# One exponential and four small transposes placed later in the queues of a four-layer graph kernel

## The chip, the cores and the metric

The kernel runs on one core of a Trainium2 chip. The metric is the device time of one execution in microseconds (us). Before the change three runs gave 1911.79, 1900.36 and 1915.36 us, a median of 1911.79. The profile is one execution more, of 1882.29 us. Line numbers (L1753) are those of the kernel before. PE is TensorE, DVE VectorE, ACT ScalarE, POOL GpSimd, and SP SyncE, which issues most of the transfers.

## The reference

A matrix `x` of 2708 rows (nodes) and 256 columns goes through four layers, each a graph part and a feed-forward part with residual additions. Two of the parts matter here.

Layer 2's graph part is attention with one head. Cut to the essentials:

```python
h = x @ W.T
a_src = (h * attn_src).sum(axis=-1)
a_dst = (h * attn_dst).sum(axis=-1)
scores = a_src[None, :] + a_dst[:, None]
mask = (adj > 0).astype(h.dtype)
s = jnp.where(scores > 0, scores, ALPHA * scores) * mask
e = jnp.exp(s - jnp.max(s, axis=1, keepdims=True)) * mask
out = (e / (jnp.sum(e, axis=1, keepdims=True) + 1e-08)) @ h
```

Its feed-forward part routes all rows to the same two of eight experts, `gelu(x @ W1 + b1) @ W2 + b2`, and normalizes the sum with `x`. Layer 3's graph part is the same kind of attention with four heads of 64 columns, and its feed-forward part one product with a bias.

## The kernel before

The rows lie in SBUF as `x`, 22 tiles of 128 rows (the last has 20). The layers follow each other, and each layer's start is worked into the end of the one before. All arithmetic is float32. The order of the work on each engine comes out of a scheduler that takes the program's order and the dependencies; `engine_after` and `in_order` (L152 to L167) add ordering edges without a wait, by which an instruction is kept behind another one of its engine. ACT, DVE, POOL and SP each work through their instructions in the order that results.

**Layer 2's front** (L1570 to L1685). The tiles are taken in groups of 2, 4, 4, 4, 4, 4 (`FOURS`). For each group:

- `turned_up` loads what layer 1's experts gave for those tiles (`mine`, transfers issued by SP), adds it to `x` (L1588, by DVE for the early groups and by POOL for tiles 14 to 21), transposes `x` on PE into a `ps_tmp` buffer of PSUM (L1596), and ACT copies that to SBUF (L1598). There are three `ps_tmp` buffers.
- `valued` multiplies by the weights (L267, into one of five `ps_acc` buffers), ACT copies the two score columns (`sc`, L1639), takes exponentials of them (L141), and DVE writes the values `hh` (L1649). The scores' tile `sc` is cleared by a memset (L1628), for the later groups on POOL.
- `row_scores` transposes the group's scores on PE (L1497), ACT copies them out (L1499), and SP stores them to DRAM (L1500).
- `row_factor` (L1507) reads them back, broadcast to all partitions (`row_read`, L1504), into the group's stretch of `Rb`, and takes the exponential of the stretch in place on ACT (L141 through `lnexp`).

The main loop (L1735 to L1778) then forms on DVE, for each tile of sources, `e = max(Rb, G) * mask` (L1745), and PE multiplies `e` with `hh` (L1753) for five columns of tiles at a time.

**Layer 2's feed-forward part and layer 3's front** (L1944 to L2055). The rows are taken in six parts: four of 512, one of 384 and one of 276. For each part, `units` runs the first products (L375, 32 matmul records per part, eight PSUM results) and the gelus on ACT (L377), and `outputs` the second products (L1962, into `ps_acc`). Between them `finish` normalizes the part before (L1978 on ACT, L1991 to L1993 on DVE). After `outputs`, `front` does layer 3's front for the part before: per tile a transpose (L220) and its copy (L221), the product with layer 3's weights (L267), and three copies on ACT (L2015, L2017, L2018), the last of which writes the scores `sc`; then `row_scores` (L1497, L1499, L1500) for the whole part. `sc` has one buffer; a memset on POOL (L2001) clears it at the beginning of each `front`. First products, transposes, weight products and score transposes all take their PSUM results from three `ps_tmp` buffers in turn.

In the last part (`end`), ACT also loads another table (L135), takes the exponentials of the first stretches of rows (`rows_of`, L1894), and scales the values (L2107); POOL copies corners of the mask (`last_mask`, L1882 to L1887). The last tiles' front is done inside the main loop of layer 3 (L2125 to L2277), whose products are L2219 and L2227 and whose weights `e` come from DVE (L2190).

Of the kernel before, what the change touches and what calls it, by code (L numbers as in the profile page):

```python
# [11 lines left out]
AF = mybir.ActivationFunctionType  # L12
# [3 lines left out]
P = 128  # L16
# [50 lines left out]
def adj_ffn4(ctx: ExitStack, tc: tile.TileContext, a: dict, out: bass.AP):  # L67
    nc = tc.nc
# [71 lines left out]
    def lnexp(out, in_, func, **kw):  # L140
        i = s.activation(out, in_, func, **kw)  # L141
        tc.add_manual_dep(i.ins, pinned[-1].ins.name, mybir.DependencyInfo(
            mybir.DependencyClass.NoSync, mybir.DependencyReason.DATA), reason="table")
# [733 lines left out]
    with ExitStack() as l0:  # L877
# [74 lines left out]
        def front(t0):  # L952

            tiles = range(t0, min(t0 + 2, NT))
            w = (len(tiles) - 1) * P + rows(tiles[-1])
            xT = gp.tile([P, DC, 2 * P], F32, name="xT", bufs=2)
            nc.sync.dma_start(xT[:, :, :w], a["xT"][:, t0 * P : t0 * P + w].rearrange(
                "(c p) t -> p c t", p=P))
            load_tiles(nc, x, tiles, a["x"])
            st = stats(tiles, by_log=True)  # L960
            for i, t in enumerate(tiles):
                r = rows(t)
                p = times(xT, i * P, r, w_sb, D)
                v.scalar_tensor_tensor(msg[:r, t, :], p, st[1][:r, i : i + 1], b_bc[:r],
                                       op0=ALU.mult, op1=ALU.add)
# [11 lines left out]
        for tiles in GROUPS:  # L977
            end = tiles is GROUPS[-1]
# [7 lines left out]
            for j in range(FULL):  # L986
# [33 lines left out]
                for p, pair in zip(acc, pairs):  # L1020
                    for n in pair:
                        if n == len(own):
                            continue
                        _, k, q = own[n]
# [477 lines left out]
    def row_read(dst, kept, h, t0, n):  # L1502

        nc.sync.dma_start(dst.rearrange("p (t c) -> p t c", c=P), kept[t0 : t0 + n, h : h + 1, :]  # L1504
                          .rearrange("t h c -> h t c").to_broadcast([P, n, P]))

    def row_factor(dst, kept, h, t0, n):  # L1507

        row_read(dst, kept, h, t0, n)
        lnexp(dst, dst, AF.Exp, scale=0.8)  # L1510

# [2 lines left out]
    with tc.tile_pool(name="t3", reuse_waits="tile", bufs=1) as t3:  # L1517
# [34 lines left out]
        with tc.tile_pool(name="g2", reuse_waits="tile", bufs=1) as gp:  # L1552
# [10 lines left out]
            def last_of(engines):  # L1563
                had = {}
                for i in nc.cur_bb.bb.instructions:
                    if i.engine in engines:
                        had[i.engine] = i.name
                return had

            def turned_up(tiles):  # L1570

                n, t0 = len(tiles), tiles[0]
                adder = v if t0 < FOURS[4][0] else g
                xT = gp.tile([P, DC, W], F32, name="xT4", bufs=2)
                late = [t for t in tiles if t not in EARLY]
                if late:
                    o = gp.tile([P, 4, D], F32, name="mine", bufs=2)
                    for i in load_tiles(nc, o, late, given[1], t0):
                        behind(i, scattered["given1"])

                def add_two(k):
                    r = rows(t0 + k + 1)
                    for q, m in (((P, 2),) if r == P else ((P, 1), (r, 1))):
                        i = k if q == P else k + 1
                        if t0 + i in EARLY:
                            continue
                        xs = x[:q, t0 + i : t0 + i + m, :]
                        adder.tensor_tensor(xs, xs, o[:q, i : i + m, :], ALU.add)  # L1588

                def turn_two(k):  # L1590
                    r = rows(t0 + k + 1)
                    p = ps_tmp()
                    for i in range(2):
                        q = rows(t0 + k + i)
                        for c in range(DC):
                            te.transpose(p[:, (c * 2 + i) * P : (c * 2 + i) * P + q],  # L1596
                                         x[:q, t0 + k + i, c * P : (c + 1) * P], ident[:q, :q])
                    s.copy(xT[:, :, k * P : (k + 1) * P + r],  # L1598
                           p.rearrange("p (c t) -> p c t", c=DC)[:, :, : P + r])

                def scale():
                    return prepared[t0] if t0 in prepared else stats(tiles, by_log=True)[1]

                for k in range(0, n if len(late) == n else n - len(late), 2):
                    add_two(k)
                    turn_two(k)
                if len(late) in (0, n):
                    rstd = scale()
                    return tiles, xT, lambda i, r: rstd[:r, i : i + 1]

                def add_late():
                    first = len(nc.cur_bb.bb.instructions)
                    for k in range(n - len(late), n, 2):
                        add_two(k)
                    engine_after(first, mybir.EngineType.DVE, last_put[0])

                def turn_late():
                    had, first = last_of(fronts), len(nc.cur_bb.bb.instructions)
                    for k in range(n - len(late), n, 2):
                        turn_two(k)  # L1620
                    for e in fronts:
                        engine_after(first, e, had[e])

                return tiles, xT, (n - len(late), add_late, turn_late)
# [30 lines left out]
                return sc, t0, n  # L1655

            ahead, todo = [turned_up(FOURS[0])], list(FOURS[1:])
            for k in range(len(FOURS)):
                sc, t0, n = valued(*ahead.pop(0))
                had, first = {}, len(nc.cur_bb.bb.instructions)  # L1660
                if ahead and type(ahead[0][2]) is tuple:
                    tiles, xT, (m, _, turn_late) = ahead[0]
                    some = prepared[tiles[0]]
                    begun = scores_of(tiles)
                    begin_values(tiles, xT, lambda i, r: some[:r, i : i + 1], *begun, 1)
                    turn_late()
                    first = len(nc.cur_bb.bb.instructions)
                    others = stats(tiles[m:], by_log=True)[1]
                    engine_after(first, mybir.EngineType.DVE, last_put[0])

                    def rstd(i, r):
                        return some[:r, i : i + 1] if i < m else others[:r, i - m : i - m + 1]

                    ahead[0] = (tiles, xT, rstd, begun)
                    begin_values(tiles, xT, rstd, *begun, len(tiles))
                    had, first = last_of(fronts), len(nc.cur_bb.bb.instructions)
                while todo and len(ahead) < 2:
                    ahead.append(turned_up(todo.pop(0)))
                    if len(ahead) == 1:
                        row_scores(kept, sc[:, :n, 1], t0, n)  # L1680
                for e, past in had.items():
                    engine_after(first, e, past)
                if k > 0:
                    row_scores(kept, sc[:, :n, 1], t0, n)
                row_factor(Rb[:, t0 * P : (t0 + n) * P], kept, 0, t0, n)  # L1685

            spread_out(hh[:, FULL, :])
            spread_out(G[:, FULL, :])
# [223 lines left out]
        with tc.tile_pool(name="h2", reuse_waits="tile", bufs=2) as hp:  # L1912
# [35 lines left out]
            def units(c0, w):  # L1948
                hT = []
                for k in range(2):  # L1950
                    h = hp.tile([P, H2C, W], F32, name="hT", bufs=2)
                    i = hidden(h, xnT, w1[:, k], lambda f: b1s[:, k, f : f + 1], c0, w, H2C)
                    hT.append(h)
                return hT, i
# [71 lines left out]
            def at_once(steps):  # L2026
                for _ in steps:
                    pass

            was = None  # L2030

            parts = CHUNKS[:-2] + [(CHUNKS[-2][0], 3 * P), (CHUNKS[-2][0] + 3 * P, W + CHUNKS[-1][1] - 3 * P)]
            for c0, w in parts:
                own = tiles_of(c0, w)
                end = c0 + w == N
                hT, i = units(c0, w)
                if end:


                    pin(i.ins.name)  # L2040
                    rows_of(0, "both")
                    last_mask()
                    factors(0, was[0][0][0])
                if was is not None:
                    at_once(finish(*was, end))
                y = ypool.tile([P, 4, D], F32, name="y", bufs=2)
                outputs(own, hT, y)
                if was is not None:
                    at_once(front(was[0]))
                    for t in range(NT) if was[0][0][0] == 0 else ():  # L2050
                        r = rows(t)
                        g.tensor_copy(mask[:, t, t * P : t * P + r], diag[:, t, :r])
                if end:
                    factors(was[0][0][0], own[0][0])
                was = (own, y)  # L2055
# [262 lines left out]
```

## Time and profile before

| what | us |
|---|---|
| median of three runs | 1911.79 |
| the profiled execution | 1882.29 |
| its span | 1880.6 |
| PE busy | 1820.4 |
| DVE busy | 1076.1 |
| ACT busy | 656.0 |
| POOL busy | 387.3 |
| layer 2's front, first transpose to first L1753 | 1062.95 to 1095.48 |
| layer 2's main loop | 1095.48 to 1308.02 |
| feed-forward part with layer 3's front, first L375 to first L2219 | 1324.04 to 1507.69 |
| layer 3's main loop from its first L2219 | from 1507.69 |

A line of the timeline gives the start, the duration, the engine, the line of the kernel and the operation, what is written and what is read, and in brackets how long the engine had been idle before it and what ended that. Matmuls of one kind that follow each other are merged (x8), and L267 or L375 count four records per result. A line of the windows gives, for a stretch of time, how long each engine was busy, and at its end the granted clock of PE as a share of full speed, the share of time in which the transfer engines were busy, and GB/s. Times are counted from the span's start.

### The profile page before, as it was taken

What the parts mean: (1) busy time and instruction counts of PE and PEld (TensorE: products, weight loads), DVE (VectorE), ACT (ScalarE), POOL (GpSimd) and SP (SyncE); (2) the same over time, 40 slices, a digit from 0 to 9 for tenths busy, and PEclk for the clock granted to TensorE, in tenths of its full rate; (3) what the DMA queues carried; (4) which work ended last, traced back from release to release, by engine and by line L of the source; (5) the groups of instructions that cost most, each with busy time, mean ns of one, the idle gap of its engine ahead of it and who ended that gap; (6) DMA issues with size and microseconds to landing.
All of it is one profiled execution on the core that took longest, in us unless ns stands there. A gap on an engine that the chain in (4) does not pass through costs nothing. (4 is left out here: it accounts for less than half of the span.)

```text
span 1880.6 us, 25848 instructions
## 1 busy us (share of the span) xinstructions
PE 1820.4 (97%) x9453; PEld 1335.0 (71%) x9453; DVE 1076.1 (57%) x2468; ACT 656.0 (35%) x1474; POOL 387.3 (21%) x460
## 2 busy tenths in 40 slices
PE   8999999999999999999999899998899999999998
PEld 7888788888888888888788788887566733233344
DVE  7687863444333525354642465555445498888877
ACT  8868742222222303113232323223223551132232
POOL 0014254333331001403547310000000100011020
PEclk9999999999998999999999999999899999999999
DMA  8535657877873554544775430000101000022120
GB/s 269 157 104 161 225 177 283 336 301 281 305 272 108 165 150 119 146 113 130 218 235 166 140 70 7 1 1 1 45 1 34 18 1 24 23 28 35 26 35 18
DMA packets 92494, 231.63 MB, mean 123 GB/s; under 512 B 18207, under 2 KB 48967, under 8 KB 84936
## 3 DMA queue, kind: packets, MB, share of 16 engines
q1 hardware_dynamic: 70792, 183.28, 29.8%
q0 software_dynamic: 21568, 46.61, 8.9%
q8 instruction: 78, 1.28, 0.3%
q14 instruction: 56, 0.46, 0.1%
HBM read 218.39 MB, written 30.80 MB: 133 GB/s over the span
## 5 line engine op out<-in xcount | busy, mean ns | idle before, releaser
L2190 DVE SCALAR_TENSOR_TENSOR e<-arena,G,mask 128x1024 f32<-128x1024 f32 (+1 forms) x252 | 275.1, 1151 | 34.1 <-PE den L2227 33.2
L2219 PE MATMUL num<-e,wh 128*64 128x512 f32 (+4 forms) x1056 | 214.1, 549 | 0.7 <-ACT L_gnn_W L1499 0.3
L1753 PE MATMUL ps_acc<-hh,e 128*128 128x257 f32 x882 | 199.2, 382 | 1.7 <-ACT o L1696 1.7
L1025 PE MATMUL acc<-msg,wt 128*128 128x256 f32 x882 | 197.8, 381 | 1.5 <-DVE wt L975 1.2
L1421 PE MATMUL acc<-sup,adrow 128*128 128x256 f32 x882 | 198.3, 382 | 0.7 <-DMA adrow<-in_adjT 0.4
L1421 PEld LDWEIGHTS acc<-sup,adrow 128*128 128x128 f32 x882 | 165.1, 190 | 28.4 <-issue 5.5
L1753 PEld LDWEIGHTS ps_acc<-hh,e 128*128 128x128 f32 x882 | 164.0, 191 | 29.0 <-ACT o L1696 4.3
L1025 PEld LDWEIGHTS acc<-msg,wt 128*128 128x128 f32 x882 | 165.5, 191 | 26.7 <-DVE wt L975 1.8
L615 PE MATMUL ps_acc<-xTs,wa 128*128 128x256 f32 (+1 forms) x768 | 169.9, 374 | 2.8 <-DVE xTs L605 2.7
L617 ACT ACTIVATE hTs<-ps_acc,wa 128x256 f32<-128x256 f32 (+1 forms) x192 | 88.8, 464 | 237.7 <-PE yacc L649 155.6
L649 PE MATMUL yacc<-wb,hTs 128*128 128x256 f32 x736 | 170.6, 384 | 0.1
L615 PEld LDWEIGHTS ps_acc<-xTs,wa 128*128 128x128 f32 x768 | 137.2, 191 | 29.0 <-DVE xTs L605 5.1
L2219 PEld LDWEIGHTS num<-e,wh 128*64 128x64 f32 (+1 forms) x1056 | 70.2, 136 | 122.7 <-issue 105.4
L649 PEld LDWEIGHTS yacc<-wb,hTs 128*128 128x128 f32 x736 | 138.8, 192 | 18.1 <-DVE ys L651 0.5
L1745 DVE SCALAR_TENSOR_TENSOR e<-Rb,G,mask 128x640 f32<-128x640 f32 (+2 forms) x110 | 85.0, 774 | 90.5 <-PE ps_acc L1753 90.4
L1386 DVE TENSOR_SCALAR mask<-adrow 128x1024 uint8<-128x1024 f32 (+1 forms) x66 | 41.6, 630 | 124.1 <-DMA adrow<-in_adjT 123.7
L2227 PE MATMUL den<-e,wh 128*32 128x512 f32 (+4 forms) x1056 | 112.2, 546 | 0.0
L221 ACT COPY xT<-ps_tmp 128x256 f32<-128x256 f32 x76 | 26.8, 366 | 199.1 <-PE ps_tmp L220 198.7
L782 PE MATMUL yacc<-wb,hTs 128*128 128x256 f32 x384 | 90.0, 390 | 0.0
L975 DVE SCALAR_TENSOR_TENSOR wt<-adrow,wt 128x640 f32<-128x640 f32 (+3 forms) x67 | 71.2, 1065 | 25.1 <-ACT wt L141 24.8
L2227 PEld LDWEIGHTS den<-e,wh 128*32 128x32 f32 (+1 forms) x1056 | 33.2, 109 | 73.6 <-issue 69.5
L537 POOL DMA_INDIRECT given<-ys,xs x46 | 65.3, 1420 | 84.0 <-DVE ys L652 68.2
(487 smaller groups left out, 2632.6 us busy)
## 6 DMA issues: line engine op xcount, KB each, us to landing
adhalf<-in_adjT SPq DMA_DIRECT2D x42, 677.0 KB
wb<-in_L_ffn_W2p SPq DMA_DIRECT2D x24, 1152.0 KB
wb<-in_L_ffn_Wdp SPq DMA_DIRECT2D x24, 1152.0 KB
wa<-in_L_ffn_W1b SPq DMA_DIRECT2D x24, 1028.0 KB
adrow<-in_adjT SPq DMA_DIRECT2D x42, 512.0 KB
adrow<-in_adjT SPq DMA_DIRECT2D x42, 320.0 KB
adrow<-in_adjT SPq DMA_DIRECT2D x21, 576.0 KB
adrow<-in_adjT SPq DMA_DIRECT2D x21, 448.0 KB
```

What stands on the lines that cost most here:

```text
L615: i = te.matmul(p[:, f % 2, : m * P], lhsT=w1[:, c, f * P : (f + 1) * P], rhs=xT[:, c, : m * P], start=(c == 0), stop=(c == DC - 1))
L617: s.activation(hT[:, f, : m * P], p[:, f % 2, : m * P], AF.Gelu, bias=bias[:, f : f + 1])
L649: te.matmul(q[:, k, :], lhsT=hT[:, f, k * P : (k + 1) * P], rhs=w2[:, f, :], start=(f == 0), stop=(f == HC - 1))
L782: te.matmul(q, lhsT=hT[:, f, :], rhs=w2[:, f, :], start=(f == 0), stop=(f == HC - 1))
L975: v.scalar_tensor_tensor(wt, ad, 1.0, wt, op0=ALU.is_lt, op1=ALU.mult)
L1025: te.matmul(p[:q, n - pair[0], :], lhsT=wt[:, k : k + q], rhs=msg[:r, j, :], start=(j == 0 and n == pair[0]), stop=(j == FULL - 1 and n == ...
L1421: te.matmul(p[:q, n - pair[0], :], lhsT=ad[:, k : k + q], rhs=sup[:, jj, :], start=(jj == 0 and n == pair[0]), stop=(jj == FULL - 1 and n ...
L1745: i = v.scalar_tensor_tensor(e[:r, :w], Rb[:r, c0 : c0 + w], G[:r, j, :], mask[:r, j, c0 : c0 + w], op0=ALU.max, op1=ALU.mult)
L1753: te.matmul(p[:, : D + 1], lhsT=e[:, k : k + q], rhs=hh[:, j, :], start=(j == 0), stop=False)
L2190: v.scalar_tensor_tensor(e[:, :w], slow[:, m % 2, k, :w], G[:, j, 2 * pair + k, :], mask[:, j, c0 : c0 + w], op0=ALU.max, op1=ALU.mult)
L2219: te.matmul(num[k * DK : (k + 1) * DK, hf, :q], lhsT=wh[some, j, 2 * pair + k, :DK], rhs=e[some, :q], start=(j == 0), stop=(j == FULL), ti ...
L2227: te.matmul(den[z * Q : (z + 1) * Q, :q], lhsT=wh[some, i, 2 * pair + k, DK : DK + 1] .to_broadcast([some.stop - some.start, Q]), rhs=e[so ...
```

## The change

Two places are edited. In layer 2's front, `row_factor` is dissolved: the read of a stretch stays where it was, and its exponential is issued after the next group's `row_scores` (the last group's after the loop). An ordering edge keeps it behind the ACT instruction that was last in the program by then.

In layer 3's front, the generator `front` is run for the part before only up to its last step, the score transpose with its copy and store. That step is run in the next part, after `units`, and an ordering edge keeps the transpose behind the last of `units`' products on PE. In the last part the step is run at once as before, so that it is moved for four of five parts.

```diff
-    def row_factor(dst, kept, h, t0, n):
-
-        row_read(dst, kept, h, t0, n)
-        lnexp(dst, dst, AF.Exp, scale=0.8)
...
             ahead, todo = [turned_up(FOURS[0])], list(FOURS[1:])
+            factor = []
+
+            def factors_of(dst):
+                had, first = last_of(fronts), len(nc.cur_bb.bb.instructions)
+                lnexp(dst, dst, AF.Exp, scale=0.8)
+                engine_after(first, mybir.EngineType.Activation, had[mybir.EngineType.Activation])
+
             for k in range(len(FOURS)):
...
                 if k > 0:
                     row_scores(kept, sc[:, :n, 1], t0, n)
-                row_factor(Rb[:, t0 * P : (t0 + n) * P], kept, 0, t0, n)
+                for f in factor:
+                    factors_of(f)
+                factor = [Rb[:, t0 * P : (t0 + n) * P]]
+                row_read(factor[0], kept, 0, t0, n)
+            factors_of(factor[0])
...
-            was = None
+            was, scored = None, None
...
                 hT, i = units(c0, w)
+                if scored is not None:
+                    at = len(nc.cur_bb.bb.instructions)
+                    done = max(k for k, z in enumerate(nc.cur_bb.bb.instructions)
+                               if z.engine == mybir.EngineType.PE)
+                    done = nc.cur_bb.bb.instructions[done].name
+                    at_once(scored)
+                    engine_after(at, mybir.EngineType.PE, done)
+                    scored = None
                 if end:
...
                 outputs(own, hT, y)
                 if was is not None:
-                    at_once(front(was[0]))
+                    scored = front(was[0])
+                    for _ in range(len(was[0]) + 1):
+                        next(scored)
+                    if end:
+                        at_once(scored)
```

## The prediction

> **What bounds the kernel now.** I read the page, then the PE, ACT and POOL timelines around the two edited places, then busy times by window for the clock.
>
> ```profile
> span 1880.6 us, 25848 instructions
> ...
> PE 1820.4 (97%) x9453; PEld 1335.0 (71%) x9453; DVE 1076.1 (57%) x2468; ACT 656.0 (35%) x1474; POOL 387.3 (21%) x460
> ```
>
> PE is busy for all but 60.2 us. An edit that removes no PE work can gain only from those gaps and from time at a lowered clock. In layer 2's front the ACT timeline shows one gap:
>
> ```profile
> 1071.89 0.58 ACT L1598 COPY xT<-ps_tmp 128x512 f32<-128x512 f32 x1 [0.31 <-PE ps_tmp L1596]
> 1076.76 0.42 ACT L141 ACTIVATE Rb<-Rb 128x256 f32<-128x256 f32 x1 [4.29 <-DMA Rb<-rows]
> ...
> 1078.63 1.05 ACT L1598 COPY xT<-ps_tmp 128x512 f32<-128x512 f32 x2
> ```
>
> ACT stands 4.29 us at the first stretch's exponential, whose rows have not landed. Queued behind it are the score copies, exponentials and turned-tile copies of later groups. PE pays:
>
> ```profile
> 1075.70 0.27 PE L1497 MATMUL ps_tmp<-ident,sc 128*4 128x128 f32 x1
> 1079.33 1.09 PE L1596 MATMUL ps_tmp<-ident,x 128*128 128x128 f32 x4 [3.36 <-ACT xT L1598]
> ```
>
> The three ps_tmp buffers are full until L1598 empties one. Then the clock (window; PE, PEld, DVE, ACT, POOL busy; PEclk, DMA share, GB/s):
>
> ```profile
> 1074.76:1078.17 3.41, 1.21 (x9) 0.74 (x8) 1.93 (x9) 1.34 (x6) 1.75 (x2) 1.00 0.24 74
> 1078.17:1081.58 3.41, 2.25 (x9) 1.99 (x10) 3.11 (x12) 2.20 (x8) 0.74 (x1) 0.50 0.41 115
> 1081.58:1085.00 3.42, 3.42 (x11) 2.78 (x10) 1.33 (x7) 1.42 (x6) 2.63 (x5) 0.50 0.31 64
> ```
>
> After a window with PE 35% busy, two windows run at half clock. POOL decides what comes next:
>
> ```profile
> 1076.42 2.48 POOL L1588 TENSOR_TENSOR x<-x,mine 128x512 f32<-128x512 f32 x2 [6.61 <-DMA mine<-given]
> 1082.37 1.27 POOL L1588 TENSOR_TENSOR x<-x,mine 128x512 f32<-128x512 f32 x1 [3.46 <-PE ps_tmp L1497]
> 1083.57 0.11 POOL L1628 MEMSET sc<- 128x8 f32 x1
> 1083.63 1.40 POOL L1588 TENSOR_TENSOR x<-x,mine 128x256 f32<-128x256 f32 x2
> ```
>
> Layer 3's front, one of four alike:
>
> ```profile
> 1384.01 2.24 PE L267 MATMUL ps_tmp<-w_l,xT 128*128 128x264 f32 x8
> 1387.39 0.27 PE L1497 MATMUL ps_tmp<-ident,sc 128*16 128x128 f32 x1 [1.14 <-issue]
> 1387.50 1.02 PE L375 MATMUL ps_tmp<-arena,w 128*128 128x512 f32 x2
> ```
>
> ```profile
> 1386.86 0.28 ACT L2017 ACTIVATE wh<-ps_tmp,rs_y 128x4 f32<-128x4 f32 x1
> 1387.00 0.28 ACT L2018 ACTIVATE sc<-ps_tmp,rs_y 128x4 f32<-128x4 f32 x1
> ```
>
> The page names no releaser ("issue"), but the turn starts 0.11 us after the last score copy ends at 1387.28, as it does in the fourth part (1482.83, then 1482.94). So it waits for ACT, with the next part's products behind it.
>
> **The Trainium skill.** "TensorE: Matmul & The Clock Gate", Part 1 (The HAM clock gate), says the clock is halved after an idle window of about 3.4 us and restored after a busy one, and that the windows run freely. The trace agrees on 3.41 us and 0.50, but not on "idle": windows 34%, 35% and 38% busy were followed by half clock; those at 60% and above mostly were not. Between lies unknown ground. The same page, Architectural detail, says ACT and DVE queues are strict FIFO; the 4.29 us above is that. "Perfetto Trace Analysis", Tensor Engine Instruction, says PE ends are estimates; so I price gaps by starts. In an unbroken row the next group starts 0.17 us before the modelled end (L375 1353.30 + 13.90 = 1367.20, L1962 at 1367.03).
>
> **Part 1, layer 2.** The instruction orders of both kernels give the same work. Of six exponentials only the first changes place on ACT: it goes behind the next group's two L1598 and its L1499. DVE, POOL and SP keep their order here. Step by step:
>
> 1. ACT after 1072.47: the score copy of tile 7, then the logarithm of the late tiles' variance, which needs DVE's mv (1073.55 + 0.30 = 1073.85). The last product of tiles 6 to 9 ends at 1074.54. In before, the stretch from the exponential's end of issue (1077.09) to the first L1598 (1078.63) takes 1.54 us; after the last product about 0.75 of it remains, so L1598 starts near 1075.3 and its first copy ends near 1075.9.
> 2. PE is free at 1075.97 but the next turn (tiles 14, 15) reads x after POOL's first add, 1076.42 + 1.26 = 1077.68. It starts near 1077.75, not 1079.33: the wait is 1.8 us, not 3.36. POOL waits for a load, which nothing here moves.
> 3. Tiles 16, 17 follow after POOL's 1078.90, then L267 of tiles 10 to 13 (14 at the 0.227 us that 18 of them took from 1067.14 to 1071.23: 3.2 us) to about 1082.9. Tiles 18 to 21 need POOL's later adds, whose load was issued at 1078.93 when POOL finished: 1083.64 and 1085.03. So the row-score turn at 1087.58 comes at about 1085.3. One half-clock window before 1082 costs 1.7 us there, most of it hidden under this POOL wait.
> 4. ACT: tile 10's score copy needs POOL's memset, 1083.68, as before. It reaches the second exponential near 1085.15. Those rows were asked for at 1082.68; two later 256 KB reads took 3.2 and 3.35 us, so they land at about 1085.9: a new wait of 0.8 us. Behind it on ACT stand the copies of tiles 18 to 21, the next L1499 and the score copies of tiles 14 to 17; PE's turn for those tiles waits for the last of them. The next two exponentials meet their rows almost at once. The turn at 1091.79 comes at about 1089.9, and the loop's first L1753 (1095.48) at about 1093.7.
>
> Part 1: -1.8 us. Bounds: about 0 if those rows land only at 1087.6 (ACT did not wait for them there) or if one window halves after 1085, where PE leads (3.41 / 2 = 1.7 us); +1.6 if two do; -3.4 if POOL holds nothing. The moved exponential itself (0.42 us) fits into ACT's idle time until 1078.3; without that cover it costs 0.42.
>
> **Part 2, layer 3.** Four turns (L1497), four copies (L1499) and four stores of rows (L1500) move behind the next part's 16 products; the fifth is not moved. A turn takes 0.11 us of PE wherever it stands. Gaps removed: 1.14 + 1.08 + 1.08 + 0.92 = 4.22, plus 4 x 0.17 = 0.68 for the overlap: 4.9 us. Is the new first product free? Its ps_tmp buffer is the last turned tile's, emptied by L221 at 1385.04. The second and third take those of the last two score products, read until 1386.62 and 1387.28 and wanted near 1387.8 and 1389.5. At its new place the turn needs a buffer emptied two products earlier. L1499 now follows the last gelu; in the first three parts 13 us of ACT idle time hide it. In the end part L1499 stands before the table load, on the chain that ends in PE's 0.94 us wait for xT at 1502.64: +0.16; one L2107 (0.25) moves off that chain ahead of L1978 and one comes back ahead of L221: about 0. Stores: the first two now issue near 1401 and 1434, so turn 0's reads (1423.61) go to about 1435, still 57 us ahead of their exponential at 1492.49. The fourth store falls behind the read that SP issued at 1490.21; its reader is a later turn. The last sc memset moves behind POOL's corner copies and ends near 1497.1; ACT writes sc at 1504.42.
>
> Part 2: -4.9 + 0.2 + 0.1 for what I have missed = -4.6 us. Bounds: 0 (a new wait takes the place of all four) and -5.1; above 0 only by rival E.
>
> **Sum.** -6.4 us: the profiled execution, 1882.3 (span 1880.6 plus 1.7), would take 1875.9. The runs shown are longer (1900.4 to 1915.4, median 1911.8), so from the median: 1905.
>
> **Rivals.** (B) The layer 2 stall only changes its name: POOL and the rows' landing hold everything. For it: steps 2 to 4 each end on a wait that stays. Against: L267 of tiles 10 to 13 ran at half clock before POOL was done. Only part 2: 1907. (C) Layer 3's gap returns at the first products because they wait for ACT as well, so the move does nothing: 1910. Against: the emptying times above. (D) The lost clock comes back whole as well (6.8 us at half clock are 3.4 us) and POOL's load is earlier: -10, 1902. (E) Slower: the second and third products of a part now wait for L2015, L2017 and L2018 of the last tiles, behind L1978 (0.6 us each) in ACT's queue. Slack is 1.2 us; a copy 1.2 + 1.3 (removed) + 0.45 (a quarter of part 1) = 2.95 us later than now makes the kernel slower, each further us costing 4: with 3.5 us, +2.2, 1914. Against: nothing in the change delays these copies.
>
> **Numbers.** A (the sum) 0.55, B 0.2, C 0.08, D 0.12, E 0.05. The cases lie between 1902 and 1914; three runs of one kernel lie 15 us apart, so a median can fall some 12 below or 4 above its place: 1889 to 1917. The likeliest case alone: 1893 to 1909. One per cent (19 us) is about what a measurement of this kernel can tell from no change; no case reaches it, and only scatter gives the sides anything: faster 0.06, within 0.91, slower 0.03.
>
> **What would show it.** Right: ACT's 4.29 us wait gone, L1596 at about 1077.7 behind POOL, a short new ACT wait for Rb near 1085, L1753 starting near 1093.7; no PE gap ahead of L1497, and L375 straight behind L267 four times. Wrong: L1596 still near 1079, half clock past 1085, a gap at L375's second product, or L2219's first product moved by less than 5 us from 1507.69.

## The result and the profile after

The kernel after takes 1902.85 us (median of 22 runs, 1899.09 to 1912.42), the kernel before beside it 1910.59 us (22 runs, 1900.36 to 1915.44). The ratio is 0.997 with a 95% interval of 0.9958 to 0.9982, that is -5.7 us (-8.0 to -3.4). The forecast was -6.4 us and 1905. By the prediction's bound of 1% the kernel is the same; the small gain is still clear of zero.

Lines of the kernel after: L1596 is now L1591, L1598 is L1593, L1588 is L1583, L1628 is L1623, L1639 is L1634, L1753 is L1759, L1962 is L1968, L2018 is L2024, L2219 is L2237. L267, L375, L1497 and L1499 keep their numbers. First the head of the page after.

```profile
span 1897.7 us, 25855 instructions
...
PE 1823.2 (96%) x9453; PEld 1334.0 (70%) x9453; DVE 1074.8 (57%) x2468; ACT 655.3 (35%) x1474; POOL 388.6 (20%) x460
```

This span is 17.1 us longer than the 1880.6 of before, although the kernel is faster. The profiled execution of before, 1882.29 us, lies below all of its 22 runs (1900.36 at least), so the two profiles seem to come from different sittings (a sitting is a group of runs made one after the other on one chip); and the time of layers 0 and 1 differs between sittings for one and the same kernel, as the last section shows. So the spans say nothing here. What can be compared are stages that start and end at the same instruction. The starts are read from the PE timeline of every run:

| stage (us) | before | after |
|---|---|---|
| layers 0 and 1, to the first L1596 | 1062.95 | 1085.43 |
| layer 2's front, to the first L1753 | 32.53 | 30.75 |
| layer 2's loop, to the first L375 | 228.56 | 228.56 |
| first group of L375 | 15.45 | 16.87 |
| from there to the first L2219 | 168.20 | 163.32 |
| the rest | 372.91 | 372.77 |

The first group of L375 is told apart because the clock is at half when it begins. Over the study it was longer wherever part 1 was in the kernel: 15.36 to 15.52 us in the four profiles without part 1 (15.37 with part 2 alone), 15.84 to 16.87 in the eight with it (15.84 with part 1 alone). Both kernels once more, below, show how that can come about. The places that were edited gain 32.53 - 30.75 = 1.78 and 168.20 - 163.32 = 4.88 us, in sum 6.66; the first group is 1.42 us longer. The part that was not touched, layer 2's loop and the rest, agrees to 0.14 us.

Layer 2's front in the ACT timeline of after:

```profile
1097.97 1.19 ACT L1593 COPY xT<-ps_tmp 128x512 f32<-128x512 f32 x2
1099.05 0.25 ACT L1499 COPY L_gnn_W<-ps_tmp 4x128 f32<-4x128 f32 x1
1099.46 0.42 ACT L141 ACTIVATE Rb<-Rb 128x256 f32<-128x256 f32 x1 [0.16 <-DMA Rb<-rows]
...
1108.97 0.63 ACT L141 ACTIVATE Rb<-Rb 128x512 f32<-128x512 f32 x1 [0.86 <-DMA Rb<-rows]
```

The exponential now stands behind both copies and L1499, and its wait of 4.29 us is down to 0.16. At the second stretch ACT has a new wait of 0.86 us for its rows. PE in the same stretch:

```profile
1098.37 0.27 PE L1497 MATMUL ps_tmp<-ident,sc 128*4 128x128 f32 x1
1100.43 0.66 PE L1591 MATMUL ps_tmp<-ident,x 128*128 128x128 f32 x4 [1.79 <-POOL x L1583]
...
1102.76 4.39 PE L267 MATMUL ps_acc<-w_l,xT 128*128 128x258 f32 x14
1106.99 1.04 PE L1591 MATMUL ps_tmp<-ident,x 128*128 128x128 f32 x8
...
1112.49 0.27 PE L1497 MATMUL ps_tmp<-ident,sc 128*4 128x128 f32 x1 [0.32 <-ACT sc L1634]
...
1116.18 0.70 PE L1759 MATMUL ps_acc<-hh,e 128*128 128x257 f32 x2
```

The wait of 3.36 us for ACT has become one of 1.79 us for POOL. POOL in turn stood for a load:

```profile
1099.12 2.49 POOL L1583 TENSOR_TENSOR x<-x,mine 128x512 f32<-128x512 f32 x2 [6.82 <-DMA mine<-given]
1104.96 1.27 POOL L1583 TENSOR_TENSOR x<-x,mine 128x512 f32<-128x512 f32 x1 [3.36 <-DMA mine<-given]
```

The windows of after, columns as in the prediction (the last three: clock, share of transfer engines, GB/s):

```profile
1094.83:1098.25 3.42, 3.18 (x18) 2.28 (x17) 3.23 (x12) 2.10 (x10) 0.00 (x0) 1.00 0.94 324
1098.25:1101.66 3.41, 1.49 (x10) 0.79 (x8) 3.41 (x14) 1.98 (x5) 2.49 (x2) 1.00 0.02 7
1101.66:1105.07 3.41, 3.41 (x11) 2.86 (x12) 1.26 (x8) 1.04 (x4) 0.10 (x1) 0.51 0.37 122
1105.07:1108.48 3.41, 3.41 (x21) 2.89 (x20) 1.46 (x4) 1.62 (x10) 2.69 (x6) 0.99 0.23 77
```

One window at half clock instead of two, again behind a window in which PE worked only a part of the time (1.49 of 3.41 us). While the load is under way, in the first line, the transfer engines are busy 94% of the time.

Layer 3's front, the same place as in the prediction and its next:

```profile
1406.13 2.24 PE L267 MATMUL ps_tmp<-w_l,xT 128*128 128x264 f32 x8
1408.21 13.90 PE L375 MATMUL ps_tmp<-arena,w 128*128 128x512 f32 x32
1421.94 0.27 PE L1497 MATMUL ps_tmp<-ident,sc 128*16 128x128 f32 x1
1422.05 13.98 PE L1968 MATMUL ps_acc<-w,hT 128*128 128x256 f32 x64
...
1524.32 0.27 PE L1497 MATMUL ps_tmp<-ident,sc 128*12 128x128 f32 x1 [0.92 <-issue]
```

L375 starts 2.08 us after L267's eight, that is 0.16 before their modelled end, so there is no gap; all 32 of its records run on without a break; the turn sits behind them and costs 0.11. The fifth turn, which was not moved, keeps its 0.92 us.

### The profile page after: what moved, and what is told of

It is laid out like the page before. It is cut to its first block, busy times and chain, and to the rows that moved or that the text cites. A ratio compares the mean times of both kernels' runs of the same rounds, so it can differ in the third digit from the quotient of the medians.

```text
span 1897.7 us, 25855 instructions
## 1 busy us (share of the span) xinstructions
PE 1823.2 (96%) x9453; PEld 1334.0 (70%) x9453; DVE 1074.8 (57%) x2468; ACT 655.3 (35%) x1474; POOL 388.6 (20%) x460
## 3 DMA queue, kind: packets, MB, share of 16 engines
q1 hardware_dynamic: 70792, 183.28, 30.4%
## 4 chain that ended last, share of the span: by engine, by line
PE 55%; DVE 4%; DMA 4%; issue 2%; ACT 2%; POOL 1%; another core or an unknown queue 0%; POOLq 0%; DVEq 0%; SPq 0%; ACTq 0%
PE num L2237 10%; PE ps_acc L1759 9%; PE acc L1421 8%; PE ps_tmp L375 8%; PE den L2245 6%; PE ps_acc L1968 3%; PE ps_tmp L267 3%; PE yacc L782 2%; DMA adrow<-in_adjT 1%; DMA hs<-hid,names 1%; DVE e L2208 1%; PE ps_tmp L220 1%; PE ps_tmp L1243 1%; PE ps_acc L708 1%; DMA mine<-given 0%
## 5 line engine op out<-in xcount | busy, mean ns | idle before, releaser
L2237 PE MATMUL num<-e,wh 128*64 128x512 f32 (+4 forms) x1056 | 214.0, 549 | 0.7 <-DVE e L2208 0.5
L1759 PE MATMUL ps_acc<-hh,e 128*128 128x257 f32 x882 | 199.2, 382 | 1.7 <-ACT o L1702 1.7
L1759 PEld LDWEIGHTS ps_acc<-hh,e 128*128 128x128 f32 x882 | 163.7, 190 | 29.2 <-ACT o L1702 4.3
L2237 PEld LDWEIGHTS num<-e,wh 128*64 128x64 f32 (+1 forms) x1056 | 70.0, 136 | 122.8 <-issue 105.0
L975 DVE SCALAR_TENSOR_TENSOR wt<-adrow,wt 128x640 f32<-128x640 f32 (+3 forms) x67 | 71.2, 1064 | 25.1 <-ACT wt L141 23.4
L537 POOL DMA_INDIRECT given<-ys,xs x46 | 65.5, 1425 | 91.9 <-DVE ys L652 78.1
```

The source lines that it names most:

```text
L1759: te.matmul(p[:, : D + 1], lhsT=e[:, k : k + q], rhs=hh[:, j, :], start=(j == 0), stop=False)
L2237: te.matmul(num[k * DK : (k + 1) * DK, hf, :q], lhsT=wh[some, j, 2 * pair + k, :DK], rhs=e[some, :q], start=(j == 0), stop=(j == FULL), ti ...
```

## The experiments

All stages are from each run's own PE timeline. "From L1962" is the time from layer 3's first second product to the first product of its loop.

**Part 1 alone.** The kernel after with layer 3's hunk undone.

```diff
-                    scored = front(was[0])
-                    for _ in range(len(was[0]) + 1):
-                        next(scored)
-                    if end:
-                        at_once(scored)
+                    at_once(front(was[0]))
```

> Only layer 2's exponential is moved; layer 3's front as before. Theory (the two parts are separate gains): the stretch from the first transpose of layer 2's front to the first product of its main loop takes 30.75 us as in the changed kernel, not the 32.53 of before, with a wait for POOL of about 1.8 us in place of the 3.36 for ACT; layer 3's front (first L375 to first L2219, with the time at half clock taken out) is unchanged, with four gaps of about 1.1 us. Time 1.8 us under before. Rival (the gain of layer 2 is an accident of the clock's windows in one profile): 32 us or more.

1906.74 against 1907.86 us, ratio 0.9996 (0.9983 to 1.0009): -0.8 us, -3.2 to +1.7. The front took 30.71 us; layer 3 kept its gaps (1.14, 1.08, 1.08, 0.92) and its 168.24. PE's timeline:

```profile
1103.08 0.66 PE L1591 MATMUL ps_tmp<-ident,x 128*128 128x128 f32 x4 [1.81 <-POOL x L1583]
...
1104.91 3.22 PE L267 MATMUL ps_acc<-w_l,xT 128*128 128x258 f32 x14
1109.07 1.17 PE L1591 MATMUL ps_tmp<-ident,x 128*128 128x128 f32 x6 [0.94 <-POOL sc L1623]
```

No window of this front ran at half clock: the 14 records took 3.22 us, against 4.39 in after. Yet the front is no shorter than after's 30.75. What the clock gave, PE stood waiting for POOL's memset (0.94), which lies behind POOL's adds, and these wait for loads.

**Part 2 alone.** The kernel after with layer 2's hunk undone (`row_factor` back in its place).

```diff
-                for f in factor:
-                    factors_of(f)
-                factor = [Rb[:, t0 * P : (t0 + n) * P]]
-                row_read(factor[0], kept, 0, t0, n)
-            factors_of(factor[0])
+                row_factor(Rb[:, t0 * P : (t0 + n) * P], kept, 0, t0, n)
```

> Only layer 3's score turns are moved. Theory: layer 2's front keeps its 3.36 us wait and takes about 32.5 us; in layer 3's front the four gaps are gone and it is 4.9 us shorter than before at equal clock. Time 4.9 us under before. Rival (the parts need each other): less than 3 us in layer 3's front.

1901.95 against 1907.86 us, ratio 0.9959 (0.9945 to 0.9974): -7.8 us, -10.5 to -5.0. The stage from L1962 took 163.34 us, 4.86 less than before's 168.20. That is just outside the interval of the times; the trace counts an edited stage by itself, whereas the times also carry the scatter of layers 0 and 1, so the 4.9 is taken for the size. In layer 2 the old wait is there again:

```profile
1107.12 0.63 PE L1596 MATMUL ps_tmp<-ident,x 128*128 128x128 f32 x4 [3.36 <-ACT xT L1598]
```

The front took 31.50 us, one less than before's 32.53, with the same wait but only one window at half clock. So the number of such windows goes with 1 us of scatter in the front of the old order; the second profile of before, below, has two again and 32.52 us.

**The score copy first.** The kernel before with the three copies of layer 3's front in another order.

```diff
                     one = y[:r, :1]
+                    s.activation(sc[:r, i, :], p[:, D + NH :], AF.Copy, scale=one)
...
-                    s.activation(sc[:r, i, :], p[:, D + NH :], AF.Copy, scale=one)
```

> The kernel before, with ACT's three copies of each tile in layer 3's front in another order: the scores first (they were the last of the three). Theory (the turn L1497 waits for the last score copy on ACT): the copy of the last tile ends earlier by the two copies that stood ahead of it, 0.36 + 0.15 = 0.5 us, so each gap before L1497 shrinks from 1.1 to about 0.6 us, five gaps, 2.5 us in all. Rival (the gap is PE's own turn-around after a weight product, or a wait for a PSUM buffer, which all three copies free): gaps unchanged at 1.1 us.

One run, 1907.52 us. The five gaps fell from 1.14, 1.08, 1.08, 0.92, 0.92 to what the PE timeline now shows, and the releaser has a name:

```profile
1414.04 0.27 PE L1497 MATMUL ps_tmp<-ident,sc 128*16 128x128 f32 x1 [0.65 <-ACT sc L2015]
1447.77 0.27 PE L1497 MATMUL ps_tmp<-ident,sc 128*16 128x128 f32 x1 [0.61 <-ACT sc L2015]
1481.48 0.27 PE L1497 MATMUL ps_tmp<-ident,sc 128*16 128x128 f32 x1 [0.60 <-ACT sc L2015]
1508.18 0.27 PE L1497 MATMUL ps_tmp<-ident,sc 128*16 128x128 f32 x1 [0.45 <-ACT sc L2015]
1531.87 0.27 PE L1497 MATMUL ps_tmp<-ident,sc 128*12 128x128 f32 x1 [0.45 <-ACT sc L2015]
```

They sum to 2.76 instead of 5.14 us, and the stage from L1962 took 165.86 us, 2.34 less than before's (what follows it was 0.5 longer). The turn waits for the score copy, as the prediction read from 0.11 us of distance where the page said only "issue". A wait for a PSUM buffer, or a cost of PE itself, would not have moved with the order of the copies.

**Three buffers for the loads.** The kernel after with one more buffer for `mine`.

```diff
-                    o = gp.tile([P, 4, D], F32, name="mine", bufs=2)
+                    o = gp.tile([P, 4, D], F32, name="mine", bufs=3)
```

> The changed kernel with three instead of two buffers for the loads of layer 1's results, so that SP issues the load of tiles 14 to 17 at once and does not hold the load of tiles 18 to 21 until POOL is done. Theory (PE's remaining wait is for POOL, and POOL's for its load): POOL's first add starts at least 1.5 us earlier against the first transpose, PE's wait of 1.79 us for POOL falls to under 0.5, no window at half clock follows, and the front takes 27 to 29.5 us instead of 30.75. Rival (the wait for POOL only hides another one, for ACT or the variance): another wait takes its place and the front stays within 0.5 us of 30.75. A third view: the loads share the transfer engines, the first of them lands later, and PE waits for DVE's add of tiles 8 and 9 instead.

The theory fell, and the third view came true. One run, 1898.89 us, front 30.54. Both of POOL's loads were asked for earlier and POOL ran through all its adds in one piece, but the first add came no earlier: 1099.56 - 1085.37 = 14.19 us after the first transpose (after: 13.69). POOL's timeline:

```profile
1099.56 5.08 POOL L1583 TENSOR_TENSOR x<-x,mine 128x512 f32<-128x512 f32 x5 [7.31 <-DMA mine<-given]
```

PE waited 1.73 us for it, and 0.80 more ahead of that for DVE, which now stood 0.75 for its own load. From 1094.80 to 1098.20 the transfer engines were busy all the time (share 1.01; 0.95 in the same stretch of after). That the earlier load took its neighbours' share of them fits this, but one run does not show it alone.

**Both kernels again, in another sitting.** No edit.

> The kernel before once more, for a second profile of its stages. Theory (the 32.53 us of layer 2's front hold two windows at half clock, and how many fall there is chance): the wait of 3.36 us for ACT is there again, and the front takes 32.5 us with two such windows or about 31.5 with one; the 22 us by which the first profile was faster in layers 0 and 1 do not come again. Rival: the same times as in the first profile, to 0.3 us in the front and 3 us in layers 0 and 1.

> The changed kernel once more. Theory: front 30.7 to 30.8 us whether a window at half clock falls into it or not, because POOL and the landing of the second stretch's rows set its end; layer 3's front, from the end of the first part's first products to the first product of the main loop, 163.3 us as in its first profile, against 168.2 of before; ratio to before about 0.997. Rival: the front varies with the clock as that of before does.

Before 1880.61 us (24 runs, 1876.84 to 1886.82), after 1873.58: ratio 0.9964 (0.9953 to 0.9975), -6.8 us (-8.8 to -4.7). A third pair, beside the later weights further down, gave 0.9968 (0.9955 to 0.9981). The expectation that the first profile of before was a lucky one fell: in this sitting its 1880 us is the median. Of the 23.7 us between the spans of after's two profiles (1897.7 and 1874.0) 22.9 lie in layers 0 and 1 (1085.43 and 1062.57; in before here 1058.67); the loop takes 228.35 and the rest 372.85 as ever. The front: 32.52 in before, 30.43 in after, 31.35 in the third pair's after.

This pair also shows what can become of a gain in the front. PE's timeline of before at the first group of L375:

```profile
1319.54 15.68 PE L375 MATMUL ps_tmp<-arena,w 128*128 128x512 f32 x32 [0.63 <-DMA w<-in_L_ffn_W]
1335.06 13.98 PE L1962 MATMUL ps_acc<-w,hT 128*128 128x256 f32 x64
```

and of after:

```profile
1321.38 16.70 PE L375 MATMUL ps_tmp<-arena,w 128*128 128x512 f32 x32 [0.66 <-DMA w<-in_L_ffn_W]
1337.91 13.98 PE L1968 MATMUL ps_acc<-w,hT 128*128 128x256 f32 x64
```

The half clock that began ahead of this group lasted to 1322.99 in before and to 1326.88 in after, in both 264.3 us after the front's first transpose. The kernel after reached the group 2.06 us sooner and so spent 5.50 us of it at half clock instead of 3.45. Its group, counted to the first second product, took 16.53 us instead of 15.52: about half of the 2.09 us that the front had gained was lost again.

**Later weights, and the fifth turn.** The kernel after, with the next part's weights (0.55 MB, requested by POOL at 1086.64 to 1091.46 in after, while `mine` is being loaded) requested behind POOL's last memset of the front, and with the fifth turn moved into layer 3's loop.

```diff
-        wr = mat(tp, "L2_ffn_Wr", E)
...
+        def late_loads(past):
+            begin = len(nc.cur_bb.bb.instructions)
+            g.dma_start(wr, a["L2_ffn_Wr"].rearrange("(c p) n -> p c n", p=P))
...
+            engine_after(begin, mybir.EngineType.Pool, past)
...
-                    if end:
-                        at_once(scored)
...
-            scores, active, waiting = {}, [], [(1, last_stretch()), (19, centred())]
+            scores, active, waiting = {}, [], [(0, scored), (1, last_stretch()), (19, centred())]
```

> The changed kernel with two more moves. First, POOL's seven loads of layer 2's and 3's weights and biases (0.55 MB) are issued after its additions of layer 1's results instead of before, so that they do not share the transfer engines with the loads that those additions wait for. Second, the fifth score turn of layer 3's front goes behind the first four products of the main loop. Theory: POOL's first addition starts 1 to 2 us earlier against the first transpose (13.69 us in the changed kernel), PE's wait of 1.8 us for POOL shrinks by as much, the front takes 29 to 30 us; and the fifth gap (0.92 us, with 0.34 behind it) goes, so that layer 3's front is 1.0 to 1.3 us shorter. Together 2 to 3 us under the changed kernel. Rival for the first: the landing is set by latency or by the order in which the loads are issued, not by shared bandwidth: POOL's first addition starts within 0.3 us of 13.69. Rival for the second: the main loop's first product waits for ACT anyway, and the front's end does not move.

1873.87 us, ratio 0.9964 (0.995 to 0.9978), the same as the kernel after beside it. In the stages both edits work, and both are paid back. POOL's first add came 71.85 - 60.52 = 11.33 us after the first transpose, PE's wait for it fell to 0.36, and the front took 28.68 us. But the loop grew by 1.9 to 230.34. ACT's timeline names it:

```profile
1090.70 0.63 ACT L141 ACTIVATE Rb<-Rb 128x512 f32<-128x512 f32 x1 [2.98 <-DMA Rb<-rows]
```

and PE's timeline the price:

```profile
1089.20 0.70 PE L1763 MATMUL ps_acc<-hh,e 128*128 128x257 f32 x2
1091.76 0.27 PE L1497 MATMUL ps_tmp<-ident,sc 128*4 128x128 f32 x1 [1.85 <-ACT sc L1637]
```

The weights now went out at 1082.09 to 1085.81, ahead of the rows asked for at 1086.00. ACT stood for these rows with the score copies behind it: the very pattern that part 1 had removed, at a later exponential. The fifth turn gained only 0.9 (from L1962 162.43), because 0.87 us of its wait stays, for ACT and now ahead of the loop's first product; the rest is 0.7 longer.

**The weights behind the last rows.** As the run before, without the fifth turn; the first of the loads also waits for the last stretch of rows.

```diff
-            g.dma_start(wr, a["L2_ffn_Wr"].rearrange("(c p) n -> p c n", p=P))
+            i = g.dma_start(wr, a["L2_ffn_Wr"].rearrange("(c p) n -> p c n", p=P))
...
+            behind(i, [read.ins])
```

> The kernel after, with the next part's weights (0.55 MB) requested only behind the landing of the last stretch of rows of layer 2's front; nothing else is changed. Theory (the front is held by loads that share the transfer engines): POOL's first add again comes about 11.3 us after the first transpose instead of 13.7, the front takes about 28.7 us instead of 30.4 to 30.8, and since no weights are in flight when the last rows are read, ACT's wait of 2.98 us and PE's wait of 1.85 us in the loop do not come back: loop 228.4, layer 3's front from the second products 163.3, 1.7 to 2.1 us under the kernel after in the profile; ratio to the kernel before about 0.9955. Rival 1 (the loss in the loop came from the order of the work, not from shared engines): loop near 230.3 again and no net gain. Rival 2: the weights now arrive too late for their first readers in the loop, and the loop or the feed-forward part is longer by a new wait.

1901.44 against 1883.72 us: ratio 1.0097 (1.0083 to 1.0112), 18 us longer in four runs. The second rival. PE's timeline:

```profile
1099.65 2.98 PE L1764 MATMUL ps_acc<-hh,e 128*128 128x257 f32 x13
1124.26 0.99 PE L1742 MATMUL ps_tmp<-L_ffn_Wr,all_ones 128*128 128x8 f32 x4 [21.62 <-DMA L_ffn_Wr<-in_L_ffn_Wr]
```

Only the 8 KB router weights waited; the scheduler sent the other loads out ahead of them (1085.42 to 1088.39). These 8 KB, asked for at 1101.11, landed 23 us later, beside a transfer of 2 MB that SP had begun at 1096.76. PE's queue holds their product early in the loop, so everything behind it stood, and the clock stayed at half for 23.9 us: loop 253.23. The front did gain: POOL's first add at 11.44 us, the front 29.68.

**Only the large weights behind.** Layer 3's weights, gamma and beta (0.51 MB) wait for the last rows; the small ones stay where after has them.

```diff
-        g.dma_start(wa[:, :, :D], a["L3_gnn_WT"].rearrange("(c p) n -> p c n", p=P))
...
+        def late_loads(read):
+            i = g.dma_start(wa[:, :, :D], a["L3_gnn_WT"].rearrange("(c p) n -> p c n", p=P))
+            behind(i, [read.ins])
```

> The kernel after, with only the three large loads of the next part (layer 3's weights, gamma and beta, 0.51 MB) requested behind the landing of the last stretch of rows; the router's weights and biases (36 KB) are requested where the kernel after requests them. Theory: the run before lost its 25 us only because the 8 KB router weights came in behind a 2 MB transfer, and PE's products of them stand in the main loop; so here no wait for them, the front about 28.7 to 29.2 us with POOL's first add 11.4 us after the first transpose, the loop 228.4, and the whole 1.5 to 2 us under the kernel after (ratio to before 0.9955 to 0.996). Rival: the large loads, now behind the same 2 MB transfer, are themselves too late, and DVE's products of layer 3's weights with the score vectors, first seen 40 us after the loop's start, hold DVE and with it PE: loop over 230.

1907.32 against 1904.98 us, ratio 1.0001 (0.9982 to 1.0019): no gain, the rival again. Front 29.16, loop 232.88. DVE's timeline:

```profile
1142.90 0.89 DVE L1760 SCALAR_TENSOR_TENSOR e<-Rb,G,mask 128x640 f32<-128x640 f32 x1 [1.28 <-PE ps_acc L1768]
1151.51 0.76 DVE L276 TENSOR_TENSOR o<-w_l,L_gnn_a_r 128x256 f32<-128x256 f32 x2 [7.73 <-DMA w_l<-in_L_gnn_WT]
```

The weights, asked for at 1127.91 behind the same 2 MB, came at about 1151.4; DVE stood 7.73 us and PE 2.58 behind it, and one window at half clock followed (1.7 us): together 4.3 of the 4.5 us by which the loop is longer than after's. The neighbour of the run before, the kernel after once more:

> The kernel after once more, as the neighbour of the run with the later weights: front 30.4 to 30.8 us, loop 228.4, layer 3's front from the second products 163.3, ratio to the kernel before 0.9964 to 0.997.

1877.64 against 1883.72 us (ratio 0.9968, above); loop 228.41, from L1962 163.33 as expected, front 31.35 where 30.4 to 30.8 was expected, with a window at half clock from 1079.2 to 1082.6; POOL's first add came 0.4 us and its third 0.6 us later in the front than in the first profile of after.

Six of these profiles also give the price of the large loads beside `mine`: from SP's request of the load for tiles 14 to 17 to POOL's add it took 5.46, 4.87 and 5.91 us in the three profiles of after, and 3.98, 3.91 and 4.03 in the three runs whose large weights came later (5.15 to 5.41 in the two profiles of before, part 1 alone, part 2 alone and the score copy first, which have them beside it too). In the first two of these three the request itself also came 0.7 to 0.9 us earlier in the front than in after: POOL's last scatter (L537) went out 1.0 us earlier, with the router weights' request no longer ahead of it.

## Why the prediction was right

The mechanism was right in both parts. The size was right for part 2; part 1 was counted too high, and by how much for the whole kernel stays open. Times below are counted from the first transpose of the front, so that the sittings fall out.

| step | forecast | after |
|---|---|---|
| 2: L1596 of tiles 14, 15 | 14.8, behind POOL, wait 1.8 | 15.00, behind POOL, 1.79 |
| 4: ACT's new wait for rows | 0.8 | 0.86 |
| 4: row-score turn, second of the late ones | 22.35 | 22.54 |
| 4: turn of tiles 14 to 17 | 26.95 | 27.06 |
| 4: first L1753 | 30.75 | 30.75 |
| part 2, gaps and overlap | -4.9, net -4.6 | -4.88 |

*Part 1, step 2*: the ACT stall of 4.29 us was worth only 1.6 us at the next transpose, since POOL's add was the wait behind it. Part 1 alone shows it with 1.81, after with 1.79. *Step 3*, that half a clock before POOL's later adds is hidden under the wait for them, held: in all four profiles of this order the front ends 11.0 to 11.3 us after the start of POOL's third add (1104.96 in after), with one window at half clock (30.75, 31.35) and without (30.71, 30.43). In the old order it is 12.0 to 13.1. *Step 4* held to 0.2 us for PE. The 0.86 us on ACT agrees because both ends came half a microsecond later than worked out: ACT stood from 22.7 us instead of 22.2, and its rows were there at 23.5 instead of 23.0.

The agreement of 30.75 with 30.75 is better than the method. Four profiles with the old order gave fronts of 32.53, 32.52, 31.50 and 31.56 (mean 32.03), four with the new order 30.75, 30.71, 30.43 and 31.35 (mean 30.81). So part 1 is worth about 1.2 us in the front; the 1.8 was counted against a before that had two windows at half clock, where two of the four have one. The term was mis-sized by that 0.6 us: the working took one profile's windows for the kernel's. The times of part 1 alone (-0.8, -3.2 to +1.7) don't tell 1.2 from 1.8 or from nothing; the traces do, for the front.

For the whole kernel they don't. The prediction had no term for the first group of L375, which begins at half clock. From the first transpose to the end of that group the four profiles without part 1 took 276.54, 276.39, 275.23 and 275.28 us (mean 275.86), the four of the new order 276.18, 274.99, 275.34 and 275.66 (mean 275.54). Only 0.3 us of part 1 is left there, less than the profiles differ among themselves. In the second sitting half of the front's gain went that way, as shown above; whether the longer group follows from part 1 in general, or from where the windows of the clock happened to fall in these twelve profiles, is not shown.

*Part 2*: four gaps of 4.22 us and four overlaps of 0.17 came back whole, in each of the runs that had this change and nothing else there (163.32 to 163.34). The 0.2 us set aside for the end part and the 0.1 for what was missed were not needed; the wait for xT there was 0.94 us in before and 0.92 in after. The first three products found their `ps_tmp` buffers empty, as worked out: L375 runs through as 32.

*The rivals.* B (the stall only changes its name) is refuted in size, since the front does get shorter, and is right about where it ends: every wait of PE that is left there (in the four profiles of the new order) ends with an add to `x`, with the memset behind POOL's adds, or with ACT, which stood for rows. C fell with the missing gap, E with the unbroken L375. D (the lost clock comes back whole and brings more) fell with the second profile of after: no window at half clock in its front, and still 30.43. On these windows the Trainium skill, "TensorE: Matmul & The Clock Gate", Part 1 (The HAM clock gate), speaks of an idle window; here a window with PE 44% busy (1.49 of 3.41) was followed by 0.51 of the clock, so the measured ground for a drop now reaches from 34% to 44% busy. In the second profile of after PE was 56% busy in the window at that place, and no half clock followed.

The sum: 1.2 + 4.9 = 6.1 us by the two edited stages, 0.3 + 4.9 = 5.2 with the first group of L375; -5.7, -6.8 and -6.0 us by the times of the three pairs. That the forecast of -6.4 lies so near is in part luck: part 1 was counted 0.6 to 1.5 us too high, and part 2, with its two allowances, 0.3 too low.

What stays open: whether the 2 us of POOL's wait can be had at all. Later weights give them in the front and lose them in the loop, in three arrangements; the first of them ends level with the kernel after. Sending the 2 MB transfer later as well was not tried.

## What to carry to other kernels

Take a stall at the head of an in-order queue for what lies between it and the next wait of the engine that it holds up, not for its own length: 4.29 us on ACT was about 1.2 us of PE's front. Then follow what was gained into the next stages: where one begins at half clock, part of it can go again. Where a small step waits for the last copy of a group and independent products stand behind it, moving it behind them gives back the whole gap, if the buffers that those products take are already empty. Where the transfer engines were busy 94% of the time, every order of the loads that was tried here only chose which reader waits; move one away only to a stretch that is read for its own transfers and its own first readers.

## What the runs showed of the hardware

The same program took 1910.59, 1907.86 and 1904.98 us in three sittings and 1880.61 and 1883.72 in two others, with 8 to 19 us between the shortest and the longest within each. By the profiles the difference is in layers 0 and 1 (1059 to 1064 us against 1085 to 1093; the kernel after has profiles of both kinds), in which 92% of all bytes are moved; the loop and the rest agree to 0.2 us where no edit touched them. What sets it is open. The number of the chip doesn't tell it: number 2 gave 1907.86 and 1883.72, number 8 gave 1880.61 and 1904.98, and it isn't recorded whether equal numbers are the same piece. A comparison across sittings could have shown either sign.

A request of 8 KB took 23 us to land beside a running transfer of 2 MB, and one of 256 KB in the same place 23.5 us; in stretches without it reads of 256 KB took 3.2 us (two reads of rows in before) to 4.7 us (the rows beside the later weights, 1086.00 to 1090.70).
